# Layernorm moments of sixteen blocks formed by wide VectorE instructions instead of one aggregation per block, in a four-layer graph network

## The chip, the cores and the metric

The kernel runs on one core of a Trainium2 chip. A core has a matrix engine (TensorE, in the profile PE, its weight loads PEld), a vector engine (VectorE, DVE), a scalar engine (ScalarE, ACT), a general engine (GpSimd, POOL) and a synchronizing engine that issues transfers (SyncE, SP). Each engine works through its own queue in order; engines wait for each other by semaphores. The metric is the device time of one execution in microseconds (us), less is better.

## The reference

The input `x` has 8 batches of 2048 nodes with 128 channels, `adj` is a symmetric adjacency matrix of 2048 x 2048. Four layers follow one another; each normalizes its input, takes the positive part, and adds a graph attention to `x`. Layers 0, 1 and 3 are attentions with additive scores; layer 2 is an attention with four heads and dot products as scores. Layer 3 normalizes a second time, after its projection.

```python
def _layernorm(x, axis=-1, eps=1e-5):
    m = jnp.mean(x, axis=axis, keepdims=True)
    v = jnp.var(x, axis=axis, keepdims=True)
    return (x - m) / jnp.sqrt(v + eps)
...
    h = jnp.maximum(_layernorm(x, axis=-1), 0.0)
    x = x + _L0_gnn_ref(h, adj, L0_gnn_W, L0_gnn_a)
    h = jnp.maximum(_layernorm(x, axis=-1), 0.0)
    x = x + _L1_gnn_ref(h, adj, L1_gnn_W, L1_gnn_a)
    h = jnp.maximum(_layernorm(x, axis=-1), 0.0)
    x = x + _L2_gnn_ref(h, adj)
    h = jnp.maximum(_layernorm(x, axis=-1), 0.0)
    x = x + _L3_gnn_ref(h, adj, L3_gnn_W, L3_gnn_a, ...)
```

Inside layer 3, after the projection `h = x W`:

```python
        mu = jnp.mean(h, axis=-1, keepdims=True)
        var = jnp.mean((h - mu) ** 2, axis=-1, keepdims=True)
        h = (h - mu) * jax.lax.rsqrt(var + LN_EPS) * ln_gamma + ln_beta
```

So there are 4 x 8 = 32 layernorms of `x` and 8 of the projection in layer 3, each over the 128 channels of 2048 nodes.

## The kernel before

**Tiles.** The 2048 nodes of a batch are 16 blocks of 128; a block's nodes lie across the 128 partitions, its channels along the free dimension. `x` of a batch stays in SBUF through all four layers. The adjacency is turned once, at the start, into a mask `edge` of bytes, and a test chooses between the function `fast`, which all these inputs take, and a `general` one.

**Units.** One layer of one batch is a unit. Units with additive scores (`Gat`) are worked in 32 tokens: `front` (L393) lets VectorE form a product `zg` of 128 x 1024 from scores and mask (L396), `back` (L401) lets TensorE multiply eight 128-wide slices of it into the sums (L406). Units of layer 2 (`Heads`) are worked in 64 beats: `scores` lets TensorE multiply (L497) and ScalarE take exponentials of the result in two halves (L500), `mask` lets VectorE multiply them by the mask (L506, 128 x 2048), `weigh` lets TensorE sum (L514). Once the first layer-2 unit has started, the loop at L626 interleaves beats with tokens of other units, somewhat more than one token to a beat.

**Pieces.** What a unit needs before its tokens can start (statistics, normalization, transposes, projection) is cut into pieces, and `host` spreads these over the tokens of units that run earlier. In the pieces, `stats` (L282) does four blocks, `end` (L288) calls `moments`, `rows` (L292) lets ScalarE normalize four blocks with one instruction each (L298, with a second one in layer 3, L301), `turned` (L304) lets TensorE transpose them (L308), and `project` (L335) multiplies by the weights. In layer 3 `norm_stats` (L360), `norm_end` (L367) and `normed` (L372, ScalarE at L374) do the same for the second layernorm.

**The layernorm.** For each block, `statistics` (L194) issues two VectorE instructions. The first (L195) leaves six numbers for each node in `st`: count, mean and sum of squared deviations of the even channels, then the same of the odd ones. The second (L196) puts these together into mean and variance in `mv`. After sixteen blocks `moments` (L184) adds epsilon to the sixteen variances (L187, VectorE), lets GpSimd raise them to the power -1/2 (L189, `rstd`), and lets VectorE form minus mean times `rstd` (L191, `nmr`). ScalarE's rows need both, as scale and bias.

**Order.** The program order of the pieces, tokens and beats is written in Python; a scheduler then sets the order of instructions on each engine from their dependences and its own estimates. The tile pools have few buffers: three for `zg`, three for the masked exponentials `z`, and three for each tag of the pool `stat`.

Of the kernel before, what the change touches and what calls it, by code (L numbers as in the profile page):

```python
# [8 lines left out]
F32 = mybir.dt.float32  # L9
# [5 lines left out]
OP = mybir.AluOpType  # L15
# [4 lines left out]
P = 128  # L20
# [4 lines left out]
EPS = 1e-5  # L25
# [12 lines left out]
def adj_preln_d4(ctx: ExitStack, tc: tile.TileContext, x, adj, w0, a0, w1, a1, w3, a3,  # L38
# [17 lines left out]
    nc = tc.nc  # L56
    B, N, C = x.shape
    NB = N // P
# [13 lines left out]
    neg_half = const.tile([P, NB], F32, name="neg_half")  # L72
# [108 lines left out]
    nc.vector.tensor_copy(near_i, near[:, 0:1])  # L181
    prep.close()

    def moments(stat, name, mv):  # L184

        var = stat.tile([P, NB], F32, tag="var", name=f"var{name}")
        nc.vector.tensor_scalar(var, mv[:, :, 1], EPS, None, op0=OP.add)  # L187
        rstd = stat.tile([P, NB], F32, tag=f"rstd{name}", name=f"rstd{name}")
        nc.gpsimd.tensor_tensor(out=rstd, in0=var, in1=neg_half, op=OP.pow)  # L189
        nmr = stat.tile([P, NB], F32, tag=f"nmr{name}", name=f"nmr{name}")  # L190
        nc.vector.scalar_tensor_tensor(nmr, mv[:, :, 0], -1.0, rstd, op0=OP.mult, op1=OP.mult)  # L191
        return rstd, nmr

    def statistics(st, mv, rows, n):  # L194
        nc.vector.bn_stats(out=st[:, n, :], in_=rows)  # L195
        nc.vector.bn_aggr(out=mv[:, n, :], in_=st[:, n, :])  # L196

    def layer3_scores(stat, rstd, nmr, sraw):

        s = stat.tile([P, 2, NB], F32, tag="s3", name="s3")  # L200
        for k in range(2):
            nc.vector.tensor_scalar(s[:, k, :], nmr, tot3[:, k:k + 1], tot3[:, 2 + k:3 + k],
                                    op0=OP.mult, op1=OP.add)
            nc.vector.tensor_mul(sraw[:, k, :], sraw[:, k, :], rstd)
        nc.vector.tensor_add(s, s, sraw)
        return s
# [18 lines left out]
    def fast(ctx):  # L225
        stat = ctx.enter_context(tc.tile_pool(name="stat", bufs=3))
# [38 lines left out]
        class Unit:  # L265
# [11 lines left out]
            def open(self):  # L277
                self.x = X[self.b]
                self.st = stat.tile([P, NB, 6], F32, tag="st", name="st")
                self.mv = stat.tile([P, NB, 2], F32, tag="mv", name="mv")  # L280

            def stats(self, q):  # L282
                if q == 0:
                    self.open()
                for n in range(q * 4, q * 4 + 4):
                    statistics(self.st, self.mv, self.x[:, n, :], n)

            def end(self):  # L288
                self.rstd, self.nmr = moments(stat, "x", self.mv)
                self.h, self.h_t = {}, {}  # L290

            def rows(self, q):  # L292
# [18 lines left out]
        class Gat(Unit):  # L311
# [48 lines left out]
            def norm_stats(self, q):  # L360
                if q == 0:
                    self.st = stat.tile([P, NB, 6], F32, tag="st", name="sth")
                    self.mv = stat.tile([P, NB, 2], F32, tag="mv", name="mvh")
                for n in range(q * 4, q * 4 + 4):
                    statistics(self.st, self.mv, self.wh[:, n, :], n)

            def norm_end(self):  # L367
                self.rstd3, self.nmr3 = moments(stat, "h", self.mv)
                s = layer3_scores(stat, self.rstd3, self.nmr3, self.sraw)
                self.exps(s[:, 0, :], s[:, 1, :], slice(0, NB))  # L370

# [254 lines left out]
        for q in range(B * 64):  # L626
            k, s = divmod(q, 64)
# [22 lines left out]
    def general(ctx):  # L650
        stat = ctx.enter_context(tc.tile_pool(name="gstat", bufs=2))
# [28 lines left out]
        def gat(layer, xb, h):  # L680
            h_t = z_tile()
            transposed_into(lambda sl, pv: nc.scalar.copy(h_t[:, sl], pv), lambda n: h[:, n, :])
            y = big.tile([P, NB, CE], F32, name="gy")
# [6 lines left out]
                nc.scalar.copy(s[:, :, n], ps[:, 3, C:C + 2])  # L690
            if layer == 3:
                st = stat.tile([P, NB, 6], F32, tag="gst", name="gst")
                mv = stat.tile([P, NB, 2], F32, tag="gmv", name="gmv")
                for n in range(NB):
                    statistics(st, mv, y[:, n, :C], n)
                rstd, nmr = moments(stat, "gh", mv)
# [9 lines left out]
            for i in range(NB):  # L706
# [9 lines left out]
                                               op0=OP.add, op1=OP.max, accum_out=top)  # L716
# [74 lines left out]
        for b in range(B):  # L791
            xb = big.tile([P, NB, C], F32, name="gx")
            nc.sync.dma_start(out=xb, in_=x[b].rearrange("(n p) c -> p n c", p=P))
            for layer in range(4):
                st = stat.tile([P, NB, 6], F32, tag="gst", name="gst")
                mv = stat.tile([P, NB, 2], F32, tag="gmv", name="gmv")
                for n in range(NB):
                    statistics(st, mv, xb[:, n, :], n)
                rstd, nmr = moments(stat, "gx", mv)
# [17 lines left out]
    with arm.Else():  # L817
        with ExitStack() as inner:
            general(inner)
# [24 lines left out]
```

## Time and profile before

| what | value |
|---|---|
| three timed executions | 3078.59, 3083.47, 3084.39 us |
| span of the profiled execution | 3074.7 us |
| mean granted TensorE clock | 0.973 |
| VectorE, zg products (L396) | 768, 1.28 us each, 974 us |
| VectorE, masks (L506) | 512, 2.29 us each, 1168 us |
| ScalarE, exponentials (L500) | 1024, 1.12 us each, 1099 us |
| GpSimd, power in layer 3 (L189) | 8, 3.87 us each, 31 us |

A group of the profile has the line, engine and operation, the tile written and the tiles read, the shape and the count; after the bar stand the group's busy time in us and the mean length of one instruction in ns; after the second bar the idle time of the engine just before these instructions and what ended most of it. A chain of waits is found from the last instruction backwards, each time to what released it. Mean lengths of neighbouring instructions may overlap, so that the distance between their starts is shorter than their length.

### The profile page before, as it was taken

How to read it: one execution, taken by the hardware profiler on the slowest of the kernel's cores; microseconds unless marked ns; L12 is line 12 of the kernel's file. 1: busy time of each engine (PE TensorE's matmuls, PEld its weight loads, DVE VectorE, ACT ScalarE, POOL GpSimd, SP SyncE). 2: the span in 40 equal slices, each digit the busy share in tenths (PEclk: the TensorE clock that was granted, in tenths of full speed). 3: DMA queues.
4: the chain of work that ended last, by engine and by line, in shares of the span. 5: the costliest groups of instructions: out<-in, count | busy, mean ns of one | idle time of the engine just before them, and what ended most of it. 6: DMA issues, size and time to landing. Idle time of an engine off the chain costs nothing.

```text
span 3074.7 us, 50065 instructions
## 1 busy us (share of the span) xinstructions
PE 2874.4 (93%) x20412; PEld 2112.7 (69%) x20415; DVE 2549.0 (83%) x3765; ACT 1808.8 (59%) x3113; POOL 168.2 (5%) x54
## 2 busy tenths in 40 slices
PE   3699989999999999999999999999999999988977
PEld 2699936677776776777677776777767766633657
DVE  5477769888898988988798997989879889987867
ACT  2343276758566558655676556665576666678652
POOL 1000000000010010000100001000000000000000
PEclk8699999999999999999999999999999999999998
DMA  6200411211113102121111212111021111312000
GB/s 223 55 1 1 97 41 45 56 32 32 32 35 69 49 17 67 32 59 25 49 44 27 52 32 66 32 39 45 15 73 32 42 28 39 79 38 55 8 8 22
DMA packets 141999, 137.90 MB, mean 45 GB/s; under 512 B 81728, under 2 KB 115136, under 8 KB 135616
## 3 DMA queue, kind: packets, MB, share of 16 engines
q1 hardware_dynamic: 134656, 125.87, 16.4%
q0 software_dynamic: 1152, 8.39, 0.7%
q8 instruction: 162, 2.65, 0.4%
q10 hardware_dynamic: 5952, 0.35, 0.2%
q14 instruction: 77, 0.63, 0.1%
HBM read 101.01 MB, written 33.55 MB: 44 GB/s over the span
## 4 chain that ended last, share of the span: by engine, by line
PE 72%; DVE 11%; ACT 8%; POOL 4%; issue 3%; DMA 2%; ACTq 0%; SPq 0%; POOLq 0%; DVEq 0%
PE ps L406 37%; PE ps L514 15%; PE ps L497 14%; DVE z L506 4%; DVE zg L396 4%; ACT z L500 3%; POOL rstdx L189 3%; PE ps L335 3%; ACT h L298 2%; PE ps L308 2%; PE ps L390 1%; DMA raw<-in_adj_dram 1%; DVE st L195 1%; POOL rstdh L189 1%; ACT wh L374 1%
## 5 line engine op out<-in xcount | busy, mean ns | idle before, releaser
L406 PEld LDWEIGHTS ps<-y,zg 128*128 128x128 f32 x12288 | 1499.2, 193 | 277.6 <-issue 132.5
L406 PE MATMUL ps<-y,zg 128*128 128x129 f32 x12288 | 1559.8, 279 | 18.3 <-DVE zg L396 14.8
L500 ACT ACTIVATE z<-ps,shift 128x1024 f32<-128x1024 f32 x1024 | 1098.7, 1117 | 679.7 <-PE ps L497 640.2
L506 DVE SCALAR_TENSOR_TENSOR z<-z,edge 128x2048 f32<-128x2048 f32 x512 | 1168.2, 2285 | 153.1 <-ACT z L500 151.2
L396 DVE SCALAR_TENSOR_TENSOR zg<-r,cr,edge 128x1024 f32<-128x1024 f32 x768 | 973.6, 1278 | 153.9 <-PE ps L406 125.6
L497 PE MATMUL ps<-m,s 128*128 128x512 f32 x2048 | 702.3, 438 | 59.9 <-ACT z L500 32.6
L514 PE MATMUL ps<-z,v 128*32 128x512 f32 x4096 | 645.9, 607 | 12.2 <-DVE z L506 12.2
L497 PEld LDWEIGHTS ps<-m,s 128*128 128x128 f32 x2048 | 339.1, 191 | 385.0 <-ACT z L500 152.3
L298 ACT ACTIVATE h<-x,nmrx,rstdx 128x128 f32<-128x128 f32 x512 | 216.2, 490 | 143.0 <-DVE nmrx L191 127.4
L189 POOL TENSOR_TENSOR rstdx<-varx,neg_half 128x16 f32<-128x16 f32 x32 | 123.4, 3859 | 2348.3 <-DVE varx L187 2069.9
L514 PEld LDWEIGHTS ps<-z,v 128*32 128x32 f32 x4096 | 93.5, 108 | 135.4 <-issue 63.4
L195 DVE BATCH_NORM_STATS2 st<-x 128x6 f32<-128x128 f32 x512 | 126.4, 268 | 7.9 <-DMA x<-in_x_dram 7.9
L335 PE MATMUL ps<-rhs,h_t 128*128 128x130 f32 x768 | 111.9, 290 | 3.2 <-ACT z L500 2.3
L335 PEld LDWEIGHTS ps<-rhs,h_t 128*128 128x128 f32 x768 | 100.1, 201 | 15.8 <-ACT z L500 11.8
L308 PE MATMUL ps<-ident,h 128*128 128x128 f32 x512 | 85.8, 284 | 24.1 <-ACT h L298 17.5
L325 ACT COPY h_t<-ps 128x512 f32<-128x512 f32 x96 | 56.1, 584 | 83.2 <-PE ps L308 83.0
L308 PEld LDWEIGHTS ps<-ident,h 128*128 128x128 f32 x512 | 61.5, 145 | 45.7 <-issue 19.3
L196 DVE BATCH_NORM_AGGREGATE mv<-st 128x2 f32<-128x6 f32 x512 | 82.1, 168 | 0.2
L191 DVE SCALAR_TENSOR_TENSOR nmrx<-mv,rstdx 128x16 f32<-128x16 f32 x32 | 5.6, 176 | 90.2 <-POOL rstdx L189 90.2
L429 ACT ACTIVATE oe<-ps,rs 128x128 f32<-128x128 f32 x128 | 53.5, 418 | 43.8 <-DVE rs L422 43.8
L351 ACT ACTIVATE y<-ps,y 128x128 f32<-128x128 f32 x256 | 73.2, 370 | 0.0
L391 ACT COPY r<-ps 128x1024 f32<-128x1024 f32 x48 | 48.4, 1011 | 41.0 <-PE ps L390 40.8
(95 smaller groups left out, 1061.9 us busy)
## 6 DMA issues: line engine op xcount, KB each, us to landing
s<-halves SPq DMA_DIRECT2D x256, 128.0 KB, 2.7
m<-halves SPq DMA_DIRECT2D x64, 512.0 KB, 5.5
raw<-in_adj_dram SPq DMA_DIRECT2D x8, 1024.0 KB, 7.3
raw<-in_adj_dram POOLq DMA_DIRECT2D x8, 1024.0 KB, 9.3
values<-h SPq DMA_DIRECT2D x32, 256.0 KB, 2.3
halves<-hi SPq DMA_DIRECT2D x128, 64.0 KB, 1.7
halves<-lo SPq DMA_DIRECT2D x128, 64.0 KB, 1.7
v<-values SPq DMA_DIRECT2D x32, 256.0 KB, 3.4
```

The costliest lines, as they stand in the source:

```text
L189: nc.gpsimd.tensor_tensor(out=rstd, in0=var, in1=neg_half, op=OP.pow)
L195: nc.vector.bn_stats(out=st[:, n, :], in_=rows)
L196: nc.vector.bn_aggr(out=mv[:, n, :], in_=st[:, n, :])
L298: nc.scalar.activation(h, self.x[:, n, :], AF.Relu, scale=self.rstd[:, n:n + 1], bias=self.nmr[:, n:n + 1])
L308: nc.tensor.transpose(pk[:, k, :], self.h[q][:, k, :], ident)
L335: nc.tensor.matmul(pv[:, k, :C + 2], lhsT=self.h_t[q][:, k * P:(k + 1) * P], rhs=rhs, start=True, stop=True)
L396: nc.vector.scalar_tensor_tensor(z, self.r[half], self.cr[:, 0, jb:jb + 1], edge[:, jb, half * HN:(half + 1) * HN], op0=OP.max, op1=OP.mult)
L406: nc.tensor.matmul(ps[:, self.sums[half][i // 3], k * CE:(k + 1) * CE], lhsT=z[:, i * P:(i + 1) * P], rhs=self.y[:, jb, :], start=(jb == 0 ...
L497: nc.tensor.matmul(ps[:, lo + c, :], lhsT=self.S[h, jb // HB][:, at:at + P], rhs=self.M[h][:, (c2 * 2 + c) * 512:(c2 * 2 + c + 1) * 512], ...
L500: nc.scalar.activation(z[:, c2 * HN:(c2 + 1) * HN], ps[:, lo:lo + 2, :].rearrange("p b t -> p (b t)"), AF.Exp, bias=shift)
L506: nc.vector.scalar_tensor_tensor(self.z[s], self.z[s], 1.0, edge[:, jb, :], op0=OP.mult, op1=OP.mult, accum_out=self.den[:, h, jb:jb + 1])
L514: nc.tensor.matmul(ps[c * HD:(c + 1) * HD, 0, :], lhsT=self.V[h][:, jb, :], rhs=z[:, c * 512:(c + 1) * 512], start=jb == 0, stop=jb == NB - 1,
```

## The change

The aggregation per block (L196) goes, and with it the tile `mv`. `moments` gets the raw statistics of all sixteen blocks and forms from them, with instructions of 128 x 16, the sum of the two means, their difference, the square of half that difference, the sum of the two sums of squared deviations, the variance, and the variance with epsilon. The power on GpSimd and the last VectorE instruction stay; the latter takes minus one half of the sum of the means. The tile `var` has four times the size. Both functions, `fast` and `general`, use it.

```diff
-    def moments(stat, name, mv):
-
-        var = stat.tile([P, NB], F32, tag="var", name=f"var{name}")
-        nc.vector.tensor_scalar(var, mv[:, :, 1], EPS, None, op0=OP.add)
+    def moments(stat, name, st):
+
+        var = stat.tile([P, 4, NB], F32, tag="var", name=f"var{name}")
+        total, apart, square, var_ = (var[:, k, :] for k in range(4))
+        nc.vector.tensor_sub(apart, st[:, :, 1], st[:, :, 4])
+        nc.vector.tensor_add(total, st[:, :, 1], st[:, :, 4])
+        nc.vector.scalar_tensor_tensor(square, apart, 0.25, apart, op0=OP.mult, op1=OP.mult)
+        nc.vector.tensor_add(var_, st[:, :, 2], st[:, :, 5])
+        nc.vector.scalar_tensor_tensor(var_, var_, 1.0 / C, square, op0=OP.mult, op1=OP.add)
+        nc.vector.tensor_scalar(var_, var_, EPS, None, op0=OP.add)
         rstd = stat.tile([P, NB], F32, tag=f"rstd{name}", name=f"rstd{name}")
-        nc.gpsimd.tensor_tensor(out=rstd, in0=var, in1=neg_half, op=OP.pow)
+        nc.gpsimd.tensor_tensor(out=rstd, in0=var_, in1=neg_half, op=OP.pow)
         nmr = stat.tile([P, NB], F32, tag=f"nmr{name}", name=f"nmr{name}")
-        nc.vector.scalar_tensor_tensor(nmr, mv[:, :, 0], -1.0, rstd, op0=OP.mult, op1=OP.mult)
+        nc.vector.scalar_tensor_tensor(nmr, total, -0.5, rstd, op0=OP.mult, op1=OP.mult)
         return rstd, nmr

-    def statistics(st, mv, rows, n):
+    def statistics(st, rows, n):
         nc.vector.bn_stats(out=st[:, n, :], in_=rows)
-        nc.vector.bn_aggr(out=mv[:, n, :], in_=st[:, n, :])
...
             def end(self):
-                self.rstd, self.nmr = moments(stat, "x", self.mv)
+                self.rstd, self.nmr = moments(stat, "x", self.st)
...
             def norm_end(self):
-                self.rstd3, self.nmr3 = moments(stat, "h", self.mv)
+                self.rstd3, self.nmr3 = moments(stat, "h", self.st)
```

More of the change, by code (lines that the diff above doesn't have):

```diff
@@ L279, in open @@
                 self.st = stat.tile([P, NB, 6], F32, tag="st", name="st")
-                self.mv = stat.tile([P, NB, 2], F32, tag="mv", name="mv")
             def stats(self, q):
@@ L285, in stats @@
                 for n in range(q * 4, q * 4 + 4):
-                    statistics(self.st, self.mv, self.x[:, n, :], n)
+                    statistics(self.st, self.x[:, n, :], n)
             def end(self):
-                self.rstd, self.nmr = moments(stat, "x", self.mv)
+                self.rstd, self.nmr = moments(stat, "x", self.st)
                 self.h, self.h_t = {}, {}
@@ L362, in norm_stats @@
                     self.st = stat.tile([P, NB, 6], F32, tag="st", name="sth")
-                    self.mv = stat.tile([P, NB, 2], F32, tag="mv", name="mvh")
                 for n in range(q * 4, q * 4 + 4):
-                    statistics(self.st, self.mv, self.wh[:, n, :], n)
+                    statistics(self.st, self.wh[:, n, :], n)
             def norm_end(self):
-                self.rstd3, self.nmr3 = moments(stat, "h", self.mv)
+                self.rstd3, self.nmr3 = moments(stat, "h", self.st)
                 s = layer3_scores(stat, self.rstd3, self.nmr3, self.sraw)
@@ L692, in gat @@
                 st = stat.tile([P, NB, 6], F32, tag="gst", name="gst")
-                mv = stat.tile([P, NB, 2], F32, tag="gmv", name="gmv")
                 for n in range(NB):
-                    statistics(st, mv, y[:, n, :C], n)
-                rstd, nmr = moments(stat, "gh", mv)
+                    statistics(st, y[:, n, :C], n)
+                rstd, nmr = moments(stat, "gh", st)
                 s = layer3_scores(stat, rstd, nmr, s)
@@ L795, in general @@
                 st = stat.tile([P, NB, 6], F32, tag="gst", name="gst")
-                mv = stat.tile([P, NB, 2], F32, tag="gmv", name="gmv")
                 for n in range(NB):
-                    statistics(st, mv, xb[:, n, :], n)
-                rstd, nmr = moments(stat, "gx", mv)
+                    statistics(st, xb[:, n, :], n)
+                rstd, nmr = moments(stat, "gx", st)
                 h = big.tile([P, NB, C], F32, name="gh")
```

## The prediction, made before the changed kernel ran

> **What bounds the kernel now.** I read the page's shares and chain of waits first, then the groups of the lines touched, then the list of who waits for whom, then the timeline around one layernorm.
>
> ```profile
> PE 2874.4 (93%) x20412; PEld 2112.7 (69%) x20415; DVE 2549.0 (83%) x3765; ACT 1808.8 (59%) x3113; POOL 168.2 (5%) x54
> PE 72%; DVE 11%; ACT 8%; POOL 4%; issue 3%; DMA 2%; ACTq 0%; SPq 0%; POOLq 0%; DVEq 0%
> ```
>
> TensorE is on the ending chain for 72% of the span; VectorE, 83% busy, holds 11% of it. So most of VectorE's time has slack, and a saving counts only where the chain runs through VectorE. That is around the layernorms:
>
> ```profile
> L195 DVE BATCH_NORM_STATS2 st<-x 128x6 f32<-128x128 f32 x512 | 126.4, 268 | 7.9 <-DMA x<-in_x_dram 7.9
> L196 DVE BATCH_NORM_AGGREGATE mv<-st 128x2 f32<-128x6 f32 x512 | 82.1, 168 | 0.2
> L189 POOL TENSOR_TENSOR rstdx<-varx,neg_half 128x16 f32<-128x16 f32 x32 | 123.4, 3859 | 2348.3 <-DVE varx L187 2069.9
> L191 DVE SCALAR_TENSOR_TENSOR nmrx<-mv,rstdx 128x16 f32<-128x16 f32 x32 | 5.6, 176 | 90.2 <-POOL rstdx L189 90.2
> ```
>
> The aggregation costs 168 ns each by its duration (640 in all with the layer-3 ones, 103 us). The last row is the larger fact: the instruction that forms nmr stands in VectorE's in-order queue and waits for GpSimd's power, 90.2 us in 32 cases, 22.5 more in the eight of layer 3: 2.8 us each. ScalarE's rows wait behind it:
>
> ```profile
> ACT h L298 <- DVE nmrx L191: 127.4, 18, 23.4
> DVE zg L396 <- PE ps L406: 125.6, 147, 4.0
> ACT wh L374 <- DVE nmrh L191: 13.4, 7, 4.7
> ```
>
> One case in the timeline, columns start, length, engine, operation:
>
> ```profile
> 1279.39 2.26 DVE L506 SCALAR_TENSOR_TENSOR z<-z,edge 128x2048 f32<-128x2048 f32 x1
> ...
> 1281.57 0.17 DVE L187 TENSOR_SCALAR varx<-mv 128x16 f32<-128x16 f32 x1
> 1281.65 1.28 DVE L396 SCALAR_TENSOR_TENSOR zg<-r,cr,edge 128x1024 f32<-128x1024 f32 x1
> ...
> 1282.28 3.40 POOL L189 TENSOR_TENSOR rstdx<-varx,neg_half 128x16 f32<-128x16 f32 x1 [75.40 <-DVE varx L187]
> ...
> 1285.72 0.17 DVE L191 SCALAR_TENSOR_TENSOR nmrx<-mv,rstdx 128x16 f32<-128x16 f32 x1 [2.79 <-POOL rstdx L189]
> ...
> 1285.93 3.57 ACT L298 ACTIVATE h<-x,nmrx,rstdx 128x128 f32<-128x128 f32 x9 [2.51 <-DVE nmrx L191]
> ...
> 1289.41 2.09 ACT L500 ACTIVATE z<-ps,shift 128x1024 f32<-128x1024 f32 x2
> ...
> 1290.56 0.30 PEld L497 LDWEIGHTS ps<-m,s 128*128 128x128 f32 x2 [2.21 <-ACT z L500]
> ```
>
> ScalarE idles 2.51 us for nmr, runs nine rows, only then the exponentials, and TensorE idles 2.21 us for these. The ending chain takes this route: VectorE, power, nmr, rows, exponentials, TensorE. The power is on the chain in 30 of 40 layernorms (23 in the x form, 87.4 us; 7 in layer 3, 27.2 us), the epsilon addition before it in 27. Of the 640 aggregations only 197 are on it, with 16.6 us.
>
> **The skill.** "Perfetto Trace Analysis", Optimizing Scalar/DVE Operations: a VectorE instruction has a fixed cost of about 60 ns, the profiled duration is about twice that because the write acknowledgement overlaps the next instruction. The trace agrees in kind: an aggregation lasts 168 ns, but the next instruction starts 0.08 us after it. "VectorE: DVE Perf Modes", Rules for kernel authors: minimize the count of operations. "SBUF — State Buffer", Who interferes with whom: a VectorE instruction with two SBUF inputs and a GpSimd one that reads SBUF block each other. The trace fits: the power takes 2.90 us with nothing beside it, 3.78 with one zg, 4.78 with one mask, so VectorE's stall stays near 2.8 us whatever is put beside it. I expect the stall unchanged.
>
> **Removed.** At 889.73 us four statistics with aggregations run: two statistics, the aggregation 0.40 us after the first, then 0.08 and 0.18 in turn, in all 1.00 us to the next mask, and 0.10 for the fourth aggregation behind it: 1.10. Statistics alone are 0.40 − 0.18 = 0.22 us apart, so four take 3 × 0.22 + 0.18 = 0.84. Saved 0.26 per four, not 4 × 0.168: 160 × 0.26 = 42 us of VectorE. By the chain's share, 197/640 = 31%, 13 us of it lies on the path; the rest beside TensorE.
>
> **Added.** Six instructions of 128x16 for one: 200 net. No row shows these forms with a step of six; the nearest are L187 (170 ns, next start after 0.08) and L204 (169 ns). If nothing waits: 0.09 us. If each waits for its predecessor: an aggregation directly behind its statistics at 2974.93 starts 0.055 us after their end, so about 0.17 + 0.06 = 0.23. In the compiled order the difference, the two sums and the square stand together in most layernorms, with the two dependent ones each behind a mask or zg; I take 0.09 × 5 = 0.45 us per layernorm. On the path in 27: 12 us (ends: 27 × 5 × 0.085 = 11 and 27 × 5 × 0.23 = 31). VectorE in all: +18 us. Instruction for instruction, the change is a draw on the path: −13 + 12.
>
> **Moved.** The compiled order of VectorE shows more. Since each wide instruction waits for the one before, the scheduler fills the gaps with masks (2.2 us) and zg products (1.2). Counting these ahead of each nmr: 13 layernorms unchanged, one has one zg fewer, 12 have one or two zg more, 14 have one or two masks more, mostly with one zg. ScalarE's rows stay within two exponentials of their old place in the x form (in six layer-3 cases they fall behind one to four more), and TensorE's transposes hardly move; SyncE's and GpSimd's DMAs keep order but for five swaps. So nmr comes later for a ScalarE queue that waits for it, with exponentials behind.
>
> - x form as in the timeline above (1282, 1641, 2003, 2365 us) and at 919: one zg earlier in the queue, ScalarE already idle: full 1.2 × 5 = 6.
> - Layer 3 at 1203, 1562, 1924, 2286: one mask and one zg, 3.4 us. At 1562 ScalarE had waited only 0.58 us, and the mask must itself await exponentials; two exponentials now go ahead of the rows. Ends 0 and 3.4 (more if the mask waits); I take half, 1.7 × 4 = 6.8. At 2801 two masks, half of 4.4 = 2.2; at 2538 one, half of 2.2 = 1.1.
> - Eight others gain a mask, six of them with a zg, but are mostly not on the chain: 0 to half of 3.4 each; about 0.6, sum 5.
> - Second of a pair (1505 us and its like): two zg, but there the chain goes back to zg and TensorE: 0.
>
> Sum 21 us. With the draw: 3074.7 + 21 − 1 = 3095 for the profiled execution. The three timed runs have median 3083.47, 9 us above that span; the same 20 us gives **3104**.
>
> **Rivals.**
>
> 1. *Faster.* A zg or mask pulled ahead of the stall feeds TensorE through it. After the second nmr of a pair at 1510 TensorE idled 1.35 us for a zg; some eight stalls on the chain continue into zg or mask. 8 × 1.35 = 11, and of VectorE's net 42 − 18 = 24 us 31%, 7: about 3065. For it: VectorE is the only route around those stalls. It decides if less than a third of the 21 us shows. Against: the chain leaves nmr for ScalarE about as often.
> 2. *No change.* Path draw, slips absorbed by ScalarE's slack (59% busy): 3083. For: 443 aggregations are off the chain already. Against: 2.51 us of idleness on ScalarE before the rows.
> 3. *Larger loss.* Layer-3 and off-chain cases take 3.4 us whole, as the mask waits for exponentials held behind TensorE: 6 + 13.6 + 4.4 + 2.2 + 13.6 (half for eight) = 40, dependent waits another 10 or so: 3130.
>
> That the change doesn't do what it says is excluded: the compiled order lacks all 640 aggregations.
>
> **Numbers.** Moderate loss 0.40, larger loss 0.12, no change 0.18, faster 0.30. A measurement of this kernel tells 0.2%, 6 us, from no change. Slower 0.52, same 0.18, faster 0.30. The likeliest's own range is 3090 to 3118 (half to one and a half of its sum, plus wide instructions up to 7 us dearer). The asked range must reach both signs: 3062 to 3130.
>
> **What would show it.** No aggregation rows; statistics groups 0.84 us; VectorE's busy time 20 to 25 us lower, or near unchanged if the wide ones wait; GpSimd still 2.9 to 4.9 us, stall per nmr still 2.8 us; ScalarE's wait for nmr (127.4 + 13.4 us) up by 20 or more, TensorE's for exponentials with it. If these waits don't grow, or the chain's VectorE share falls, I am wrong and rival 1 or 2 holds.

## The result, and the profile after

The changed kernel takes **3096.45 us** (median of four, 3093.54 to 3098.31), the kernel before 3083.93 beside it (four, 3078.59 to 3087.01). The ratio is **1.0042, with a 95% interval of 1.0024 to 1.0059**: slower by 13 us. The profiled executions last 3094.3 and 3074.7 us at granted clocks of 0.972 and 0.973. The forecast was 3104, with 3095 for the profiled one.

The page after: the engines' busy time, the shares of the chain of waits, and three groups of the layernorm (line, engine, operation, shape, count; after the bar busy time and mean length in ns; then idle time before and its releaser).

```profile
PE 2898.4 (94%) x20415; PEld 2114.3 (68%) x20415; DVE 2525.5 (82%) x3325; ACT 1810.2 (59%) x3113; POOL 155.5 (5%) x54
PE 76%; ACT 8%; DVE 7%; POOL 4%; issue 3%; DMA 1%; ACTq 0%; SPq 0%; POOLq 0%; DVEq 0%
...
L201 DVE BATCH_NORM_STATS2 st<-x 128x6 f32<-128x128 f32 x512 | 111.0, 278 | 8.5 <-DMA x<-in_x_dram 8.5
L195 POOL TENSOR_TENSOR rstdx<-varx,neg_half 128x16 f32<-128x16 f32 x32 | 109.8, 3431 | 2362.3 <-DVE varx L193 1402.8
L197 DVE SCALAR_TENSOR_TENSOR nmrx<-varx,rstdx 128x16 f32<-128x16 f32 x32 | 5.6, 176 | 81.0 <-POOL rstdx L195 81.0
```

VectorE has 440 instructions fewer and is busy for 23.5 us less, and yet the kernel is longer. No row of aggregations is left. The stall of VectorE before nmr is a little smaller than before (81.0 against 90.2 us). The chain's VectorE share is not larger but smaller, 7% against 11%.

Who waits for whom, in the kernel after (engine and line, what it waited for, us in total, times, longest us):

```profile
ACT z L503 <- PE ps L500: 671.3, 394, 28.7
DVE z L509 <- ACT z L503: 165.1, 153, 9.9
DVE zg L399 <- PE ps L409: 156.9, 166, 3.6
ACT h L302 <- DVE nmrx L197: 143.3, 22, 23.6
PEld ps L500 <- ACT z L503: 140.0, 164, 4.5
ACT wh L377 <- DVE nmrh L197: 11.1, 8, 2.6
```

ScalarE's wait for nmr grew from 127.4 + 13.4 to 143.3 + 11.1 us, by 13.6. Waits among the three engines of the loop grew too: the exponentials for TensorE 31 us more than before (671.3 against 640.2), zg for TensorE 31 more (156.9 against 125.6), the masks for exponentials 14 more. These sums overlap in time and cannot be added to the loss. TensorE's weight loads wait less for exponentials (140.0 against 152.3), not more. They also wait less for zg products: 32.6 against 42.4 us, and the matmuls themselves 4.6 against 14.8. What grew on TensorE is the wait for masks: in the sums of layer 2 from 32.2 to 44.1 us (loads and matmuls together). TensorE's busy time is 24 us larger, 22 of it in the sums of layer 2 (L514 before, 645.9 us; L517 after, 668.1) with the same instructions at nearly the same clock. The Trainium skill ("Perfetto Trace Analysis", Tensor Engine Instruction (MATMUL, LD_WEIGHTS)) says that the ends of matmuls are a model in a profile and not observed; so I don't read this growth as work.

The layernorm that the prediction showed at 1282 us, in the kernel after (start, length, engine, operation; in brackets idle time before it and what ended that):

```profile
1278.95 0.87 DVE L201 BATCH_NORM_STATS2 st<-x 128x6 f32<-128x128 f32 x4
...
1279.73 1.27 DVE L399 SCALAR_TENSOR_TENSOR zg<-r,cr,edge 128x1024 f32<-128x1024 f32 x1
...
1280.91 0.18 DVE L188 TENSOR_TENSOR varx<-st 128x16 f32<-128x16 f32 x1
1281.01 0.18 DVE L189 TENSOR_TENSOR varx<-st 128x16 f32<-128x16 f32 x1
1281.11 0.18 DVE L191 TENSOR_TENSOR varx<-st 128x16 f32<-128x16 f32 x1
1281.20 0.17 DVE L190 SCALAR_TENSOR_TENSOR varx<-varx 128x16 f32<-128x16 f32 x1
1281.29 2.28 DVE L509 SCALAR_TENSOR_TENSOR z<-z,edge 128x2048 f32<-128x2048 f32 x1
...
1283.50 0.17 DVE L192 SCALAR_TENSOR_TENSOR varx<-varx 128x16 f32<-128x16 f32 x1
1283.59 1.28 DVE L399 SCALAR_TENSOR_TENSOR zg<-r,cr,edge 128x1024 f32<-128x1024 f32 x1
1284.78 0.17 DVE L193 TENSOR_SCALAR varx<-varx 128x16 f32<-128x16 f32 x1
...
1289.26 0.17 DVE L197 SCALAR_TENSOR_TENSOR nmrx<-varx,rstdx 128x16 f32<-128x16 f32 x1 [2.79 <-POOL rstdx L195]
1289.36 2.29 DVE L509 SCALAR_TENSOR_TENSOR z<-z,edge 128x2048 f32<-128x2048 f32 x1
1289.47 1.65 ACT L302 ACTIVATE h<-x,nmrx,rstdx 128x128 f32<-128x128 f32 x4 [4.42 <-DVE nmrx L197]
1291.03 2.09 ACT L503 ACTIVATE z<-ps,shift 128x1024 f32<-128x1024 f32 x2
...
1291.70 1.04 PE L517 MATMUL ps<-z,v 128*32 128x512 f32 x2 [1.65 <-DVE z L509]
```

Four wide instructions start 0.09 to 0.10 us apart; the two that need a result just made stand behind a mask and behind a zg. From the long instruction behind the last statistics to nmr it takes 9.53 us (1279.73 to 1289.26); before it was 7.60 (1278.12 to 1285.72). ScalarE idles 4.42 us for nmr instead of 2.51: 1.9 us, where the prediction had put 1.2. What TensorE waits for here is another thing than before. It idles 1.65 us for the mask that is queued on VectorE behind the late nmr; in the kernel before, its multiplications idled 1.30 us for the exponentials behind the rows. Two lines of the kernel before, for these readings:

```profile
1278.12 1.25 DVE L396 SCALAR_TENSOR_TENSOR zg<-r,cr,edge 128x1024 f32<-128x1024 f32 x1
...
1290.56 0.73 PE L497 MATMUL ps<-m,s 128*128 128x512 f32 x2 [1.30 <-ACT z L500]
```

The trace does not divide the loss among the layernorms. Already the first power starts at 89.1 us instead of 96.1. Comparing the starts of the powers, after less before, gives −7.5 us near 206 us, 0 at 833, +9.2 at 1562, +12 at 2286 and +20.0 at 2984. The profiled execution of the kernel after thus begins with a lead of 7.5 us and ends 20 behind, while the timed medians differ by 13. For sizes I go by timed ratios alone.

### The profile page after: what moved, and what is told of

The parts are those of the page before. It is cut to its first block, busy times and chain, and to the rows that moved or that the text cites. A ratio compares the mean times of both kernels' runs of the same rounds, so it can differ in the third digit from the quotient of the medians.

```text
span 3094.3 us, 49726 instructions
## 1 busy us (share of the span) xinstructions
PE 2898.4 (94%) x20415; PEld 2114.3 (68%) x20415; DVE 2525.5 (82%) x3325; ACT 1810.2 (59%) x3113; POOL 155.5 (5%) x54
## 4 chain that ended last, share of the span: by engine, by line
PE 76%; ACT 8%; DVE 7%; POOL 4%; issue 3%; DMA 1%; ACTq 0%; SPq 0%; POOLq 0%; DVEq 0%
PE ps L409 38%; PE ps L517 17%; PE ps L500 15%; ACT z L503 3%; PE ps L339 3%; POOL rstdx L195 3%; DVE z L509 2%; DVE zg L399 2%; ACT h L302 2%; PE ps L312 2%; PE ps L393 2%; POOL rstdh L195 1%; DMA raw<-in_adj_dram 1%; DVE st L201 1%; ACT wh L377 0%
## 5 line engine op out<-in xcount | busy, mean ns | idle before, releaser
L503 ACT ACTIVATE z<-ps,shift 128x1024 f32<-128x1024 f32 x1024 | 1100.5, 1117 | 700.0 <-PE ps L500 671.3
L509 DVE SCALAR_TENSOR_TENSOR z<-z,edge 128x2048 f32<-128x2048 f32 x512 | 1168.5, 2285 | 166.8 <-ACT z L503 165.1
L399 DVE SCALAR_TENSOR_TENSOR zg<-r,cr,edge 128x1024 f32<-128x1024 f32 x768 | 975.0, 1279 | 189.3 <-PE ps L409 156.9
L517 PE MATMUL ps<-z,v 128*32 128x512 f32 x4096 | 668.1, 614 | 17.1 <-DVE z L509 17.0
L302 ACT ACTIVATE h<-x,nmrx,rstdx 128x128 f32<-128x128 f32 x512 | 217.9, 493 | 152.0 <-DVE nmrx L197 143.3
L195 POOL TENSOR_TENSOR rstdx<-varx,neg_half 128x16 f32<-128x16 f32 x32 | 109.8, 3431 | 2362.3 <-DVE varx L193 1402.8
L517 PEld LDWEIGHTS ps<-z,v 128*32 128x32 f32 x4096 | 95.4, 108 | 147.9 <-issue 65.4
L201 DVE BATCH_NORM_STATS2 st<-x 128x6 f32<-128x128 f32 x512 | 111.0, 278 | 8.5 <-DMA x<-in_x_dram 8.5
L393 PE MATMUL ps<-ident,cr 128*128 128x128 f32 x384 | 55.1, 292 | 16.5 <-ACT r L394 10.4
## 6 DMA issues: line engine op xcount, KB each, us to landing
s<-halves SPq DMA_DIRECT2D x256, 128.0 KB, 2.7
```

Source lines behind the costliest of these rows:

```text
L195: nc.gpsimd.tensor_tensor(out=rstd, in0=var_, in1=neg_half, op=OP.pow)
L302: nc.scalar.activation(h, self.x[:, n, :], AF.Relu, scale=self.rstd[:, n:n + 1], bias=self.nmr[:, n:n + 1])
L393: nc.tensor.transpose(pk[:, k, :], self.cr[:, 1, n:n + 1].to_broadcast([P, P]), ident)
L399: nc.vector.scalar_tensor_tensor(z, self.r[half], self.cr[:, 0, jb:jb + 1], edge[:, jb, half * HN:(half + 1) * HN], op0=OP.max, op1=OP.mult)
L503: nc.scalar.activation(z[:, c2 * HN:(c2 + 1) * HN], ps[:, lo:lo + 2, :].rearrange("p b t -> p (b t)"), AF.Exp, bias=shift)
L509: nc.vector.scalar_tensor_tensor(self.z[s], self.z[s], 1.0, edge[:, jb, :], op0=OP.mult, op1=OP.mult, accum_out=self.den[:, h, jb:jb + 1])
```

## The experiments

Times of the kernel before differ among the occasions (medians of 3079.66 to 3083.93), so the table gives ratios to the runs of the kernel before on the same chip. The last column is (ratio − 1) x 3081 us. "Pinned" means that on VectorE each zg product and each mask is kept, in the queue too, behind the last epsilon addition that precedes it in the program. The edge used for that only orders two instructions of one engine; it asks for no semaphore.

| kernel | ratio | 95% | us against before |
|---|---|---|---|
| after | 1.0042 | 1.0024 to 1.0059 | +12.9 |
| removal alone | 0.9926 | 0.9912 to 0.9939 | −22.8 |
| addition alone | 1.0091 | 1.0077 to 1.0105 | +28.0 |
| after, pinned | 0.9941 | 0.9927 to 0.9954 | −18.2 |
| before, pinned | 0.9962 | 0.9948 to 0.9976 | −11.7 |
| addition, pinned | 0.9990 | 0.9982 to 0.9998 | −3.1 |
| after, pinned in layer 3's second layernorm only (8) | 1.0032 | 1.0020 to 1.0044 | +9.9 |
| after, pinned for `x` of layers 2 and 3 only (16) | 1.0057 | 1.0040 to 1.0074 | +17.6 |
| after, pinned for `x` of layers 0 and 1 only (16) | 1.0018 | 1.0009 to 1.0026 | +5.5 |
| after, nmr on GpSimd | 1.0055 | 1.0042 to 1.0069 | +16.9 |
| after, pinned, nmr on GpSimd | 1.0031 | 1.0020 to 1.0043 | +9.6 |
| after, five wide instructions | 1.0024 | 1.0017 to 1.0031 | +7.4 |
| after, pinned, five wide instructions | 0.9968 | 0.9958 to 0.9978 | −9.9 |

My theory was the prediction's: the dependent steps of the chain let the scheduler put masks and zg products between them, nmr comes later in VectorE's queue, and what waits for it loses about 20 us. Its main rival is that the six instructions themselves cost this time, by their length and by waiting for each other.

### One part of the change at a time

The first kernel has the aggregations gone and one instruction instead of the six. It takes mean and variance from the even channels alone and leaves the odd half of the channels out of them.

```diff
-        var = stat.tile([P, 4, NB], F32, tag="var", name=f"var{name}")
-        total, apart, square, var_ = (var[:, k, :] for k in range(4))
...
-        nc.vector.tensor_scalar(var_, var_, EPS, None, op0=OP.add)
+        var_ = stat.tile([P, NB], F32, tag="var", name=f"var{name}")
+        nc.vector.tensor_scalar(var_, st[:, :, 2], 2.0 / C, EPS, op0=OP.mult, op1=OP.add)
...
-        nc.vector.scalar_tensor_tensor(nmr, total, -0.5, rstd, op0=OP.mult, op1=OP.mult)
+        nc.vector.scalar_tensor_tensor(nmr, st[:, :, 1], -1.0, rstd, op0=OP.mult, op1=OP.mult)
```

> The aggregations are left out and nothing is put in their place: moments has one 128x16 instruction, as before, and takes mean and variance from the even channels alone, so the odd half of the channels is left out of the moments. Order theory (the loss comes from nmr standing later in VectorE's queue, because dependent wide instructions let the scheduler put masks and zg in front of it): in the compiled order nmr is here nowhere later than before and in 15 of 40 layernorms one zg earlier, so the time falls below the kernel before, by the 13 us of aggregations on the path and a few more: 3068 us (3058 to 3076). Time theory (the wide instructions cost their own time on the path, the order is idle): 3071 us, before less 13. Chance theory (start and clock): 3083 us, within 6 of before.

Measured: 3058.44 us, −22.8: at the lower edge of what the order theory wrote, more than the 13 of the prediction. In its profile nmr stands behind a zg or a mask fewer than before in 19 layernorms and never behind more. Since the order changes with it, this is not the aggregations alone; a kernel below has the order held.

The second keeps the aggregations and lets a chain of six instructions of the same kinds and dependences work on `mv`.

```diff
...
-        nc.vector.tensor_scalar(var, mv[:, :, 1], EPS, None, op0=OP.add)
+        nc.vector.tensor_sub(apart, mv[:, :, 0], mv[:, :, 1])
+        nc.vector.tensor_add(total, mv[:, :, 0], mv[:, :, 0])
+        nc.vector.scalar_tensor_tensor(square, apart, 0.0, apart, op0=OP.mult, op1=OP.mult)
+        nc.vector.tensor_add(var_, mv[:, :, 1], mv[:, :, 1])
+        nc.vector.scalar_tensor_tensor(var_, var_, 0.5, square, op0=OP.mult, op1=OP.add)
+        nc.vector.tensor_scalar(var_, var_, EPS, None, op0=OP.add)
...
-        nc.vector.scalar_tensor_tensor(nmr, mv[:, :, 0], -1.0, rstd, op0=OP.mult, op1=OP.mult)
+        nc.vector.scalar_tensor_tensor(nmr, total, -0.5, rstd, op0=OP.mult, op1=OP.mult)
```

> The aggregations stay, and the same chain of six wide instructions is put behind them (it reads the aggregated means and variances, and the result is unchanged). The compiled order puts nmr behind the same masks and zg as the changed kernel, in six layernorms behind one more mask. Order theory: before plus the loss of the order and of the instructions, some 13 us above the changed kernel because the aggregations are still there: 3110 us (3103 to 3120). Time theory: before plus five instructions in 27 layernorms at 0.09 to 0.23 us: 3096 to 3115 us. Chance theory: 3083 us.

Measured: 3108.44 us, +28.0, as the order theory had it; the time theory's range, 3096 to 3115, holds it as well. The chain alone makes the kernel slower, and more than the removal brings. It does not yet say whether by its own time or by the order, which moved further than expected: counted in the profiles over all 40 layernorms, nmr stands behind 26 masks and 34 zg products more than in the kernel before; in the kernel after it is 15 and 25.

### The order held

```diff
+    last_eps = [None]
+
+    def behind(ins):
+        if last_eps[0] is not None:
+            tc.add_manual_dep(ins.ins, last_eps[0].ins.name, mybir.DependencyInfo(
+                mybir.DependencyClass.NoSync, mybir.DependencyReason.DATA), reason="behind")
...
-        nc.vector.tensor_scalar(var_, var_, EPS, None, op0=OP.add)
+        last_eps[0] = nc.vector.tensor_scalar(var_, var_, EPS, None, op0=OP.add)
...
-                nc.vector.scalar_tensor_tensor(z, self.r[half], self.cr[:, 0, jb:jb + 1],
+                behind(nc.vector.scalar_tensor_tensor(z, self.r[half], self.cr[:, 0, jb:jb + 1],
...
-                nc.vector.scalar_tensor_tensor(self.z[s], self.z[s], 1.0, edge[:, jb, :],
+                behind(nc.vector.scalar_tensor_tensor(self.z[s], self.z[s], 1.0, edge[:, jb, :],
```

> The changed kernel, instruction for instruction, with one thing tied down: every zg and mask that is written later in the program is queued on VectorE behind the epsilon addition, so that none can be put between the wide instructions. The compiled order then has nmr where the kernel before had it, in seven layernorms one zg earlier. Order theory: the loss is gone, 3080 us (3070 to 3086), at or a little below before. Time theory: the waits between the wide instructions are now hidden by nothing, 0.14 us each in two or three places per layernorm, so it is not faster than the changed kernel: 3097 to 3110 us. Chance theory: 3083 or 3097, no statement.

Measured: 3064.11 us, −18.2 against before and −31.1 against after. With the same instructions as the kernel after, it is faster than both kernels. The theory that the six instructions cause the loss by their own time falls; the order theory holds in kind, and the gain is larger than its range (3070 to 3086). The pin does more than restore the old order: in the profile nmr stands as far back as in the kernel before in 25 layernorms, behind one zg more in one, and behind fewer zg or masks in 14, where 7 were expected. The same layernorm in the pinned kernel, timeline:

```profile
1274.72 1.28 DVE L406 SCALAR_TENSOR_TENSOR zg<-r,cr,edge 128x1024 f32<-128x1024 f32 x1
1275.92 0.18 DVE L195 TENSOR_TENSOR varx<-st 128x16 f32<-128x16 f32 x1
...
1276.21 0.17 DVE L197 SCALAR_TENSOR_TENSOR varx<-varx 128x16 f32<-128x16 f32 x1
1276.41 0.17 DVE L199 SCALAR_TENSOR_TENSOR varx<-varx 128x16 f32<-128x16 f32 x1
1276.62 0.17 DVE L200 TENSOR_SCALAR varx<-varx 128x16 f32<-128x16 f32 x1
1276.70 2.28 DVE L516 SCALAR_TENSOR_TENSOR z<-z,edge 128x2048 f32<-128x2048 f32 x1
...
1281.78 0.17 DVE L204 SCALAR_TENSOR_TENSOR nmrx<-varx,rstdx 128x16 f32<-128x16 f32 x1 [2.79 <-POOL rstdx L202]
...
1281.99 3.57 ACT L309 ACTIVATE h<-x,nmrx,rstdx 128x128 f32<-128x128 f32 x9 [1.71 <-DVE nmrx L204]
```

The whole chain takes 0.78 us (1275.92 to 1276.70) with nothing between its steps; the dependent ones start 0.20 to 0.21 us apart. From the long instruction ahead of it to nmr it takes 7.06 us instead of 9.53, and ScalarE waits 1.71 us instead of 4.42. VectorE is busy for the same time in both (2526.9 and 2525.5 us): busy time says nothing of this difference. The waits of the pinned kernel, for the rows shown of the kernel after:

```profile
ACT z L510 <- PE ps L507: 641.0, 366, 28.7
...
DVE zg L406 <- PE ps L416: 130.1, 148, 4.0
ACT h L309 <- DVE nmrx L204: 128.0, 22, 23.4
```

Three of the grown waits are back at the values of the kernel before (640.2, 125.6, 127.4). They are no measure of the loss, though: in the removal, the fastest kernel here, zg waits 156.5 us for TensorE, as long as in the kernel after.

Is the order a matter of the chain, or would any kernel gain from the pin? Two further kernels have the same `behind` at the same places, one in the kernel before (its epsilon addition on `var`, shown here), one in the addition.

```diff
-        nc.vector.tensor_scalar(var, mv[:, :, 1], EPS, None, op0=OP.add)
+        last_eps[0] = nc.vector.tensor_scalar(var, mv[:, :, 1], EPS, None, op0=OP.add)
```

> The kernel before, with its aggregations, and zg and mask tied behind its epsilon addition in the same way. The compiled order has nmr at the places of the pinned kernel in all 40 layernorms but one (there a zg earlier). So the two differ by the work alone: 640 aggregations against 200 wide instructions. Prediction's own sums (13 off, 12 on): 3065 us, as the pinned kernel. With the measured ones (12 us for the aggregations, from the addition kernel against the changed one, and 6 for the wide instructions, from the pinned kernel against removal alone): 3070 us (3066 to 3075). If the tie itself does nothing for the kernel before: 3081 us, and the pinned kernel's gain is the aggregations'.

> Aggregations and the six wide instructions together, pinned: the same instructions as the addition kernel, whose 3108 us they had with masks and zg in between. Order theory: the pinned kernel plus 12 us for the aggregations, 3076 us (3070 to 3082), some 30 below the addition kernel. Time theory: 3108 us or more.

Measured: 3069.64 us, −11.7, and 3078.16 us, −3.1; each some 2 us or less from the 3070 and 3076 that were written for order and measured prices. Now each cost can be taken at a held order:

| what | from | us |
|---|---|---|
| 640 aggregations, order free | addition less after | 15.1 |
| 640 aggregations, pinned | addition pinned less after pinned | 15.1 |
| order with the chain, aggregations there | addition less addition pinned | 31.1 |
| order with the chain, without aggregations | after less after pinned | 31.1 |
| order with one instruction | before less before pinned | 11.7 |
| five more wide instructions, pinned | addition pinned less before pinned | 8.6 |

The change is −15.1 + 8.6 + (31.1 − 11.7) = +12.9 us. That this sum is the result follows from how the differences are taken. The two rows for the aggregations agree, and so do the two for the order with the chain, but this is one agreement and not two: both come from the same four kernels. Each ratio has 3 to 5 us to a side, so a difference of two has, by the root of the sum of squares, some 4 to 7, and the 19.4 us in brackets some 8; equality to 0.1 us is chance. With the order held in both kernels, the change is a gain of 6.5 us (−18.2 against −11.7, some 6 to a side).

How much of the order is the late nmr? Here is what stands ahead of nmr in the profiles beyond what stands there in the pinned kernel with the same instructions, summed over the 40 layernorms, with masks taken at 2.2 us and zg products at 1.2 (the kernel with five instructions is described further below):

| kernel | more masks | more zg | their length, us | gain by the pin, us |
|---|---|---|---|---|
| before | 4 | 15 | 27 | 11.7 |
| five wide instructions | 13 | 20 | 53 | 17.3 |
| after | 19 | 39 | 89 | 31.1 |
| addition | 30 | 45 | 121 | 31.1 |

The cost grows with what was put ahead of nmr, and a quarter to under half of its length appears in the time. It isn't proportional. And the late nmr is not all that changes: the pin holds VectorE's queue around the layernorms only, and the scheduler arranges the other queues anew. Compared place by place, 463 of ScalarE's 3113 instructions are others in the pinned kernel than in the kernel after (395 between before and after). So "order" means the compiled order that the chain leads to, headed by VectorE's; how much of the 31 us lies in the late nmr itself and how much in what the other queues do with it, these runs don't separate. The move alone, with the instructions of the kernel before and nmr later, was not tried.

The granted clock is a rival in part. In all four pairs the pinned kernel ran at a higher one, by 0.003 to 0.0045 in the mean over its executions (0.9725 after, 0.9770 after pinned). In the 57 executions of the kernel before that were timed beside the two kernels just shown, 0.001 of clock goes with 2.2 us by a fitted line. By this estimate some 6 to 10 us of each gain go together with the clock; whether the order brings the clock about is not shown. The difference of 19.4 us between the gains of after and before is touched by 1 us only.

### Which layernorms

The pin was given to some layernorms only, by a flag; in the program nothing else changed. The lines shown are those for `x` of layers 2 and 3.

```diff
-        last_eps[0] = nc.vector.tensor_scalar(var_, var_, EPS, None, op0=OP.add)
+        eps = nc.vector.tensor_scalar(var_, var_, EPS, None, op0=OP.add)
+        if pin:
+            last_eps[0] = eps
...
-                self.rstd, self.nmr = moments(stat, "x", self.st)
+                self.rstd, self.nmr = moments(stat, "x", self.st, self.layer in (2, 3))
```

> The changed kernel with zg and mask tied behind the epsilon addition for the eight layernorms of layer 3's projection alone. The compiled order has nmr of these where it was before, those of layers 0 to 3 as in the changed kernel, but for four (at 1286 us and its like) that have a mask instead of a zg in front. By the prediction's items (7 of these layernorms cost 10 us, the four get 1 us dearer each): 3090 us (3085 to 3094). By the segments of the changed kernel's trace (from the power of layer 3 to the next power 78.9 us before and after, no loss): 3096 us (3092 to 3102).

> The same for the sixteen layernorms of x in layers 2 and 3 alone: the pairs (the second nmr of a pair stands behind two zg less than in the changed kernel), and four late ones. By the prediction's items (0 for the pairs, some 2 us for the late ones): 3095 us (3091 to 3098). By the segments of the trace (the stretch around a pair 2.9 and 3.8 us longer after the change in the first two cycles, less than 1.1 in the next two; 8.7 us lost between 2538 and 2801 us): 3077 us (3070 to 3085).

> The changed kernel with zg and mask tied behind the epsilon addition for the sixteen layernorms of x in layers 0 and 1 alone, the group that neither of the two partly pinned kernels touched. By subtraction (all pinned 32 us faster than the changed kernel, layer 3's projection alone 8 faster, layers 2 and 3 alone 3 slower, if the groups add up): 3069 us (3064 to 3075). By the prediction's items (6 us for the five with one zg, up to 5 for those off the chain): 3085 us (3080 to 3090).

Measured: layer 3's second layernorm 3088.72 us, against after −3 by ratio and within the intervals; `x` of layers 2 and 3, 3099.26, against after +5, also within them; `x` of layers 0 and 1, 3086.1, against after −7. The first and the last lie in the ranges that were written from the prediction's items, the middle one lies outside both of its ranges. The reading by stretches of the trace, which had put the loss into layers 2 and 3, falls: pinning there gains nothing. That the rest must then lie in layers 0 and 1 falls too (3069 was expected of that). The three groups give −6 us together, where the items had some −19, and all at once give −31. A pin in one group is followed by another arrangement elsewhere, and these kernels don't follow the count above: against the pinned kernel, nmr stands in the last two behind nearly the same amount more (13 masks and 21 zg products, 14 and 26), and they take 36 and 24 us longer than it. Why all three groups together keep the gain is open.

### The wait on VectorE taken away

If what costs is that VectorE stands still for GpSimd with masks queued behind, then nmr should be formed on GpSimd, right behind the power.

```diff
+        nc.vector.tensor_scalar(total, total, -0.5, None, op0=OP.mult)
...
-        nc.vector.scalar_tensor_tensor(nmr, total, -0.5, rstd, op0=OP.mult, op1=OP.mult)
+        nc.gpsimd.tensor_tensor(out=nmr, in0=total, in1=rstd, op=OP.mult)
```

> The changed kernel with nmr formed by GpSimd right behind the power (a seventh wide instruction on VectorE multiplies the sum of the means by minus one half). VectorE no longer waits for GpSimd: 103.6 us of idle time before nmr in 39 places goes, the rows on ScalarE wait for GpSimd instead, longer by one GpSimd instruction. Order theory, widened (what hurts is everything that is queued behind or before the waiting nmr on VectorE): 3060 us (3040 to 3080), below both kernels. Time theory: VectorE is on the chain for 7 percent only, so little is won and the seventh instruction is lost: 3090 to 3105 us.

Measured: 3095.91 us, +16.9, where 3060 had been expected. VectorE's stall for `x` (81.0 us after) is gone. In layer 3 it is not: there VectorE itself reads nmr next, and that instruction (`s`, L208) waits 21.7 us for GpSimd, where nmr had waited 22.6. The idle time has moved; waits of this kernel:

```profile
DVE z L510 <- ACT z L504: 186.7, 164, 9.9
DVE zg L400 <- PE ps L410: 176.0, 180, 8.7
...
DVE s L208 <- POOL nmrh L198: 21.7, 7, 3.1
```

Against 165.1 and 156.9 in the kernel after. Freed from most of its waiting for GpSimd, VectorE waits for ScalarE and TensorE instead. The theory that VectorE's own stall costs the time falls in the size written; a smaller gain could be hidden, because the 40 multiplications take 23.0 us on GpSimd against 7.0 on VectorE (0.22 to 1.97 us each in `x`, against 0.18). To see whether the order hid a gain, the same was done on the pinned kernel:

> The pinned kernel with nmr formed by GpSimd, as in e4: order of before, and no VectorE instruction that waits for GpSimd. If only the place of the power and nmr relative to ScalarE's queue counts: as the pinned kernel, 3064 us (3058 to 3070). If VectorE's stall of 2.8 us costs in itself: 3050 us (3040 to 3057). If the seventh wide instruction and GpSimd's second one cost on the path in 30 layernorms at 0.2 to 0.5 us: 3070 to 3080 us.

Measured: 3087.7 us, 27.8 more than the pinned kernel (+9.6 against −18.2) and outside all three ranges. Two of its waits:

```profile
ACT h L310 <- POOL nmrx L205: 185.0, 20, 23.6
...
PEld ps L508 <- ACT z L511: 186.8, 182, 7.2
```

ScalarE waits 185.0 us for nmr instead of the pinned kernel's 128.0, and TensorE's loads 186.8 for exponentials instead of 139.3. In its compiled order ScalarE's rows stand two exponentials earlier in 8 of the 32 layernorms of `x`; that would hold up exponentials behind rows that must wait. This is argued, not shown; the longer multiplications, 22.8 us against 7.0, account for 16 us at most.

### One link less in the chain

The sum of the squared deviations takes epsilon with it, so that five instructions and one dependence less remain; once with the pin (then tied to the fifth instruction), once without, as shown.

```diff
-        nc.vector.tensor_add(var_, st[:, :, 2], st[:, :, 5])
+        nc.vector.scalar_tensor_tensor(var_, st[:, :, 2], C * EPS, st[:, :, 5], op0=OP.add, op1=OP.add)
         nc.vector.scalar_tensor_tensor(var_, var_, 1.0 / C, square, op0=OP.mult, op1=OP.add)
-        nc.vector.tensor_scalar(var_, var_, EPS, None, op0=OP.add)
```

> The pinned kernel with five wide instructions: epsilon times 128 goes into the sum of the squared deviations. One dependent instruction less in 40 layernorms, with nothing put between: 0.09 to 0.23 us each on 27 to 33 of them. Order theory and time theory alike: 3059 us (3055 to 3063); if the wide instructions cost nothing once they are together: 3064 us.

> The changed kernel, not pinned, with five wide instructions (epsilon times 128 in the sum of the squared deviations): one link of the chain less for the scheduler to fill. In the compiled order 12 layernorms that had a mask and a zg more have the mask alone or the zg alone, and ten that had one or two zg more have none or one. Order theory: part of the loss goes, 3086 us (3078 to 3092). Time theory: 40 instructions less, 3092 to 3095 us.

Measured: pinned 3069.65 us, 8 us more than with six, at intervals that don't meet, and above both numbers written; free 3088.54, 5.5 us less than with six, where the intervals do, and in the order theory's range. Forty instructions fewer cannot cost 8 us by their time. The two pinned kernels differ in 138 of ScalarE's 3113 places, and in the layernorm near 833 us nmr stands behind one mask more and one zg less. Which of these it is stays open. It sets a measure for all the rest: an arrangement that shifts for no purpose went with 8 us here, and single items of less than that can't be attributed.

## Why the prediction was right, point by point

**Removed: −13, measured −15.1.** The four statistics of a group now take 0.78 us (1278.95 to 1279.73) where 0.84 was worked out, and VectorE's busy time fell by 23.5 us where 20 to 25 was written. That 31% of the saving lies on the path, read from the chain of waits, agrees with the 15.1; with 5 to 7 us to a side, this doesn't test it sharply.

**Added: +12, measured +8.6.** The value taken, 0.09 us each where nothing waits, is what the trace shows (0.09 to 0.10). But the term was written for the free order and measured in the pinned one. There the dependent ones take 0.20 to 0.21, near the upper price of 0.23, and the six together 0.78 us, 0.70 more than the one of 0.08 before: on the path in 27 layernorms, as predicted, 19 us. So the agreement with 12 is in part luck; why only 8.6 shows is open.

**Moved: +21, measured +19.4** (31.1 less the 11.7 that the order cost the kernel before; some 8 us to a side). This term decided the sign, and it came from counting what stands ahead of nmr in the compiled queues, not from the diff. The counts are right: the profile has 13 layernorms unchanged, 12 with zg products alone more, 14 with masks more and one with a zg less. The total held; its division did not, so that the total is in part luck. At 1282 us one zg made ScalarE wait 1.9 us more instead of 1.2. Pinning layer 3's second layernorm gave 3 us where the items had 6 net, layers 0 and 1 gave 7 for 11, layers 2 and 3 lost 5 where 2 was to be gained; and no sum over groups gives the whole. The step "two exponentials go ahead of the rows, so half" could not be tested at this size. I had also not seen that the order already cost the kernel before 12 us.

**The sum: +20, measured +13.** All three terms erred to the same side, the saving 2.1 us too small, the two costs 3.4 and 1.6 too large; together 7 us, less than the 8 us between the two pinned kernels with five and six instructions, and within the intervals. 3104 instead of 3096 needs no failed mechanism. (The lower end of the likeliest range should have been 3093, not 3090: half of the sum of 20 above 3083.) Part of the mechanism was nevertheless not as written, as the tests show.

**The tests I set.** The power (2.9 to 4.9 us written, 2.90 to 4.87 measured) was as said, and so was the stall, near 2.8 us, in 35 of the 40 layernorms; in five it was 1.6 us or less. Three tests failed. ScalarE's wait for nmr grew by 13.6 us, not "20 or more"; TensorE's wait for exponentials fell (loads and matmuls together from 184.9 to 165.3 us) instead of growing; and the chain's VectorE share fell, which I had written would make me wrong and a rival right. The measured loss and the pin speak against those rivals, so the tests did not tell what they were set for. For the exponentials one place shows a reason: a late nmr also holds back what is queued behind it on VectorE, and at 1282 us TensorE waits for that mask and not for exponentials. I had named the route through ScalarE alone. Over the span TensorE's wait for masks in the sums of layer 2 grew by 12 us, of which the pinned kernel (38.7) takes back 5; how much of the loss runs over this route is not shown. The chain's share goes with the aggregations and not with the order: it is 11% or more in all four kernels that keep them, at 3070 us (before pinned) as at 3108 (addition), and 5 to 9% in all those without, the fast pinned one too (8%). And ScalarE's wait does not follow the time: in the addition it waits 121.5 us for nmr of `x`, less than the 127.4 before, at 28 us more time.

**The rivals.** The faster rival's mechanism is in the trace: TensorE's waits for zg fell by 20 us (57.2 to 37.2, loads and matmuls), with zg products now ahead of the stall; in the pinned kernel, which keeps them behind, they are 74.4. It was outweighed, not absent. "No change" is excluded by the interval, and the larger loss too; that the masks come whole (3.4 us each in layer 3) is not borne out by the pin there.

## What to carry to other kernels

A short chain of small dependent instructions is not priced by its instructions alone: here the scheduler put long work into its gaps, and the one who waits for the end of the chain waited for that too. Count what stands ahead of the awaited instruction in the in-order queue, before and after a change. The count gave the direction, and in four pairs of kernels the cost grew with it, but not in proportion, and kernels pinned in part did not follow it. If it grew, hold the order in both kernels and measure again before judging the change itself: here the same instructions were 0.4% slower than before as the scheduler placed them, 0.6% faster once pinned, and 0.2% faster than the kernel before pinned likewise. A wait row that does not grow is no proof that its event isn't late, and neither is a chain share.

## What the runs showed that I had not expected

- Taking 82 of the 104 us of stall off VectorE, by letting GpSimd form nmr, gained nothing, and where the order was pinned the kernel became 28 us slower.
- Gains of holding the order don't add: −3, +5 and −7 us for three groups of layernorms, −31 for all.
- One dependent instruction of 128x16 starts 0.20 to 0.21 us after its predecessor, an independent one 0.09 to 0.10. The Trainium skill ("VectorE: DVE Perf Modes", The DRAIN you can't avoid) says, of a row of copies, that semaphores between them cost nothing extra; between these short instructions a dependence costs 0.11 us.
- Execution times of kernels that differ only in the arrangement of the same or nearly the same instructions reach from 3064 to 3099 us.
